# A spectral mixer and a quantised feed-forward layer on one core: the transform along h split over even and odd rows

## The chip, the core and the metric

The kernel runs on one core of a Trainium2 chip. The metric is the device time of one launch in microseconds (us). The kernel before takes 2757.5 us, the median of three runs that lie between 2753.7 and 2760.68 us. The profiled execution spans 2754.4 us, with a mean granted TensorE clock of 0.970.

The core has five instruction queues that run beside one another: TensorE (PE in the profile, with PEld for its weight loads), VectorE (DVE), ScalarE (ACT), GpSimd (POOL) and SyncE (SP), which here only issues transfers. ScalarE issues transfers too. Each queue runs in the order in which the program was written.

## The reference

The input is x with 8 images of 128 rows (h), 128 columns (w) and 96 channels. One layer is computed: a mixer in the frequency domain, then a feed-forward part in 8-bit floats, each added to its input. Cut to what matters:

```python
v = _ln_c(x)                                        # norm over the 96 channels, eps 1e-6
x_pre = soa(einsum('bhwc,mc->bhwm', v, w1))         # relu, square, scale, bias; m = 192
xf = rfft2(x_pre over h, w, norm='ortho')           # 128 x 65 frequencies
y = relu(bn(einsum('bhwc,sc->bhws', v, sp_w)))      # 48 context channels
fused = concat([v.mean(h, w), y.mean(h, w)])
r = softmax((soa(fused @ fc1.T) @ fc2.T).reshape(-1, 3, 192), axis=1)
comb = einsum('shwm,bsm->bhwm', filt, r)            # filt: three complex filters, resized from small grids
x = x + einsum('bhwm,cm->bhwc', irfft2(xf * comb), w2)

t = x as (b, 16384, 96)
h = relu(q_acc(q_acc(q_mul(ln(t)) @ q_mul(W1).T) + q_mul(b1)))   # 384 wide
y = q_acc(q_acc(q_mul(h) @ q_mul(W2).T) + q_mul(b2))
x = t + y                # q_mul: 5 exponent, 2 mantissa bits; q_acc: 5 and 10 bits
```

## The kernel before

Each image passes three streams, and the streams of neighbouring images overlap: while image b is in the last stream, b+1 is in the second and b+2 in the first.

**Stream a, `before(b)`**, goes over the columns w in 32 units of 4 columns. `load_x` brings 16 columns with h on the partitions, `measure` (L581) takes statistics per pixel, and the helper `rstd` turns them into a reciprocal root: five GpSimd steps for the variance (L591 to L595), a root on ScalarE (L600), a reciprocal on VectorE (L604), and one Newton step of four GpSimd operations (L413 to L416). `store_r` writes the factors to DRAM and `load_r` reads them back, spread over the 96 channel partitions (`rB`). `scale` (L659) multiplies the channel-major copy of x, which is stored as (c, h, w), by `rB`, and puts the product into `zT` as (c, w, h). `project` (L672) multiplies by the weights, `rectify` (L683) and `square` (L690) follow on ScalarE. `transform` (L701) is the real transform along h: for two columns at a time one product of the full 128 x 128 basis `F1` with 384 columns of `X`. `put` (L708) copies each result from PSUM with ScalarE, and `store_y` (L711) writes four columns to the DRAM tensor `Yd`, laid out as (frequency j, w, 192 channels). The order of the frequencies in `Yd` is groups of four: k, k+32 in cosine, the same in sine.

**Stream s, `spectrum(b)`**, goes over 33 groups g of four frequency rows. `load_y` reads them with w on the partitions. The 192 channels make one and a half times 128, so `pack` (L866, GpSimd) copies the last 64 channels of two rows into one tile `yb`, and `along_w` (L874) does three products for each of cosine and sine. `weigh` (L857) multiplies the resized filters by the mixing weights, `filters_of` (L887) resizes them along w in 64 x 64 tiles, and VectorE (`make` L913, `times` L916) and GpSimd (`turn_back` L923, `real_basis` L938 and L940) do the complex product. `mix_low` (L971, L984, again in 64 x 64 tiles), `mix` (L995), `mixed`, `invert` (L1011), `inverted` and `store_v` (L1021) multiply by w2, go back along w and write `Vd`.

**Stream c, `after(b)`**, goes over w again in 32 units of 4 columns, in blocks of 16. `last` (L1123) goes back along h, `residual` (L1131) adds x, `measure` and `rstd` normalise (with three more GpSimd steps for the mean, L612 to L614), `quantise` (L1151) makes 8-bit values, `turn` (L1156) and `turned` (L1166, VectorE) transpose them, `first` (L1170) makes three PSUM banks of 512, `accumulated` (L1177) copies each to 16 bits, `biased` (L1181) adds the bias and clips at zero, once for each of the three, `hidden` (L1185) rounds to 8 bits, `second` (L1192), `put8` (L1203) and `bias` (L1207) follow, and `add_up` (L1210, GpSimd) and `store` end the block. For the last image every second `quantise` runs on VectorE (L1149).

**The order.** Every piece of work is recorded by `at` with a planned time, computed from the tables `STREAMS`, `O` and `OWN` (the time of a unit plus an offset for the kind of work), and with the pieces that it needs. `in_order` sorts them by that time, moves a follower to at least a fixed `LAG` behind what it needs, and hands out six PSUM banks; a piece that needs more banks than are free is held back. The result is pinned as the order on all five engines.

Of the kernel before, what the change touches and what calls it, by code (L numbers as in the profile page):

```python
# [56 lines left out]
NG = 31  # L57
NP = 16
WB = 16
HB = WB // 2  # L60
NWB = W // WB
QW = 4
NQ = WB // QW
NU = W // QW

STREAMS = {
    "a": ((-2.3, 125.8), (125.5, 235.3), (361.7, 294.9), (654.8, 258.7), (914.4, 293.7), (1208.1, 250.0), (1549.9, 242.8), (1792.3, 246.3)),
    "s": ((145.6, 218.8), (374.7, 303.7), (677.8, 243.8), (924.7, 275.3), (1223.3, 298.2), (1520.9, 283.8), (1811.0, 258.1), (2086.7, 264.0)),
    "c": ((456.0, 260.1), (727.0, 260.5), (1018.6, 240.5), (1251.4, 323.7), (1604.0, 246.4), (1857.3, 253.2), (2101.5, 235.3), (2381.7, 138.0)),
# [4 lines left out]
        "a_load_xT": -1.97,  # L74
        "a_load_r": -5.06,
        "a_store_r": -9.58,
        "a_load_x": -10.466,
        "a_measure": -8.83,
        "a_scale": -1.29,
        "a_project_u0": 0.1,  # L80
        "a_rectify_u0": -4.22,
        "a_project_u2": 0.07,
        "a_rectify_u2": -5.38,
        "a_square": -3.56,
        "a_context": 0.88,
        "a_transform_u0": 1.37,
        "a_put_u0": 1.34,
        "a_transform_u2": 1.21,
        "a_put_u2": -5.7,
        "a_store_y": -2.773,  # L90
        "a_step": 0.26,
        "a_rstd": -4.27,
    },
    ("c", 6): {
        "c_step": 0.17,
        "c_rstd": 5.43,
        "c_quantise": 6.37,
        "c_first": 9.04,
        "c_accumulated": 8.29,
        "c_biased": 7.57,  # L100
        "c_load_v": 0.59,
        "c_last": 1.93,
        "c_residual": 1.66,
        "c_measure": -1.75,
        "c_turn": 8.21,
        "c_turned": 2.68,
        "c_hidden": 10.24,
        "c_second": 11.45,
        "c_put_blkq": 6.6,
        "c_bias": 8.21,  # L110
        "c_add_up": 7.54,
        "c_store": 8.05,
    },
    ("c", 7): {
        "c_step": 0.11,
        "c_rstd": 5.33,
        "c_quantise": 6.22,
        "c_first": 7.65,
        "c_accumulated": 2.03,
        "c_biased": 7.82,  # L120
        "c_load_v": -2.61,
        "c_last": 1.79,
        "c_residual": -0.5,
        "c_measure": -5.02,
        "c_turn": 6.63,
        "c_turned": 6.3,
        "c_hidden": 8.8,
        "c_second": 9.02,
        "c_put_blkq": 9.35,
        "c_bias": 3.04,  # L130
        "c_add_up": 9.99,
        "c_store": 3.47,
    },
    ("s", 7): {
        "s_load_y": -6.85,
        "s_load_t": -3.503,
        "s_weigh": -2.2,
        "s_pack": -2.89,
        "s_along_w_g1": -1.69,
        "s_copy_sr": -3.98,  # L140
        "s_along_w_g0": -5.22,
        "s_filters_of": -1.38,
        "s_make_dmALUsubtract": -2.12,
        "s_make_dpALUadd": -2.45,
        "s_times_t1dm00": -7.26,
        "s_times_t2dp10": -11.08,
        "s_times_t3dm01": -3.94,
        "s_times_t4dp11": -1.04,
        "s_turn_back_g0": -0.01,
        "s_turn_back_g1": -0.53,  # L150
        "s_real_basis_g0": 0.5,
        "s_real_basis_g1": -13.48,
        "s_along_w_g0_x": -1.76,
        "s_alone_z": -4.41,
        "s_filters_of_x": -1.0,
        "s_alone_t": -3.96,
        "s_alone_x": -1.27,
        "s_mix_low": 0.05,
        "s_mix": -0.12,
        "s_mixed": -3.05,  # L160
        "s_invert": 0.88,
        "s_inverted": -2.36,
        "s_store_v": -9.843,
# [3 lines left out]
T_WEIGHTS, T_CONST, T_ROWS = -112.0, -48.0, (-19.0, 94.0)  # L167

O = {
    "a_load_xT": -3.37,  # L170
    "a_load_r": -8.87,
    "a_store_r": -11.4,
    "a_load_x": -10.636,
    "a_measure": -7.71,
    "a_scale": -0.88,
    "a_project_u0": -0.28,
    "a_rectify_u0": -6.09,
    "a_project_u2": 0.13,
    "a_rectify_u2": -4.67,
    "a_square": 0.25,  # L180
    "a_context": 0.82,
    "a_transform_u0": 1.31,
    "a_put_u0": -2.63,
    "a_transform_u2": 1.05,
    "a_put_u2": -2.74,
    "a_store_y": -5.993,
    "s_load_y": -4.81,
    "s_load_t": -2.653,
    "s_weigh": -0.53,
    "s_pack": -0.19,  # L190
    "s_along_w_g1": 0.49,
    "s_copy_sr": -4.8,
    "s_along_w_g0": 0.64,
    "s_filters_of": 0.97,
    "s_make_dmALUsubtract": 0.87,
    "s_make_dpALUadd": 0.85,
    "s_times_t1dm00": -3.01,
    "s_times_t2dp10": -9.29,
    "s_times_t3dm01": -2.33,
    "s_times_t4dp11": 1.37,  # L200
    "s_turn_back_g0": 1.79,
    "s_turn_back_g1": 2.03,
    "s_real_basis_g0": 2.18,
    "s_real_basis_g1": -7.56,
    "s_along_w_g0_x": 0.15,
    "s_alone_z": -4.37,
    "s_filters_of_x": 1.5,
    "s_alone_t": -0.23,
    "s_alone_x": -3.9,
    "s_mix_low": 1.23,  # L210
    "s_mix": 1.38,
    "s_mixed": -0.75,
    "s_invert": 2.22,
    "s_inverted": 0.88,
    "s_store_v": -1.203,
    "a_step": 0.53,
    "a_rstd": -3.83,
    "c_step": 0.22,
    "c_rstd": 4.21,
    "c_quantise": 5.11,  # L220
    "c_first": 6.59,
    "c_accumulated": 5.43,
    "c_biased": 7.0,
    "c_load_v": -2.91,
    "c_last": 0.76,
    "c_residual": -1.01,
    "c_measure": 0.49,
    "c_turn": 6.04,
    "c_turned": 3.07,
    "c_hidden": 7.86,  # L230
    "c_second": 8.37,
    "c_put_blkq": 5.18,
    "c_bias": 3.81,
    "c_add_up": 8.94,
    "c_store": 3.77,
}
BANKS = 6

LAG, TRANSFER_LAG = 0.15, 2.28
# [6 lines left out]
)  # L246

# [27 lines left out]
def _constants():  # L275
# [7 lines left out]
    weight[0] = weight[L - 1] = 1.0  # L283

    rows = []
    for g in range(NG):
        k = g + 1
        rows += [k, k + 32, 64 + k, 96 + k]
    rows += [32, 96, 0, 64]

    turned = []
    for p in range(NP):
        for r in range(2):
            for g, cs in _columns(p, r):
                k = g + 1 + 32 * r if g < NG else 32 if g == NG else 64 * r
                turned.append(k + 64 * cs)
    out = {
        "F1": np.concatenate([cos, sin[1:-1]])[rows].T * norm,
# [3 lines left out]
        "CEN": np.eye(C) - 1 / C,  # L302
# [19 lines left out]

def in_order(ops):


    keys = {op.key for op in ops}
    assert len(keys) == len(ops)
    left, then, ready, held = {}, defaultdict(list), [], []
    place = {op.key: op.time for op in ops}
    for op in ops:  # L330
        needs = {k for k in op.needs if k in keys}
        left[op.key] = len(needs)
        for k in needs:
            then[k].append(op)
        if not needs:
            heappush(ready, (op.time, op.seq, op))

    free, banks, frees, order = list(range(BANKS)), {}, defaultdict(list), []
    for op in ops:
        for u in op.until:  # L340
            frees[u].append(op)
# [993 lines left out]
```

## Time and profile before

| engine | busy us | share of the span |
|---|---|---|
| PE | 2567.8 | 93% |
| PEld | 1953.0 | 71% |
| DVE | 2276.1 | 83% |
| ACT | 2233.0 | 81% |
| POOL | 2122.2 | 77% |

The transfers move 618.05 MB, 224 GB/s on the mean over the span. In the view by 40 slices PE shows 9 (90% or more busy) from the third slice to the 34th, and falls to 5 to 7 in the last three; the first slice has 4. The other engines show 6 to 9 in the middle.

A group of instructions is listed as line, engine, operation, output <- input, shapes, count | busy time in us, mean ns of one | idle time of the engine just before them, and who ended it. A product of 32-bit floats shows as two instructions. The busy time of a group is the union of its instructions, so that overlapping ones count once, while the mean counts each in full.

### The profile page before, as it was taken

How to read it: one execution, taken by the hardware profiler on the slowest of the kernel's cores; microseconds unless marked ns; L12 is line 12 of the kernel's file. 1: busy time of each engine (PE TensorE's matmuls, PEld its weight loads, DVE VectorE, ACT ScalarE, POOL GpSimd, SP SyncE). 2: the span in 40 equal slices, each digit the busy share in tenths (PEclk: the TensorE clock that was granted, in tenths of full speed). 3: DMA queues.
4: the chain of work that ended last, by engine and by line, in shares of the span. 5: the costliest groups of instructions: out<-in, count | busy, mean ns of one | idle time of the engine just before them, and what ended most of it. 6: DMA issues, size and time to landing. Idle time of an engine off the chain costs nothing.

```text
span 2754.4 us, 69406 instructions
## 1 busy us (share of the span) xinstructions
PE 2567.8 (93%) x25130; PEld 1953.0 (71%) x25130; DVE 2276.1 (83%) x5887; ACT 2233.0 (81%) x4452; POOL 2122.2 (77%) x3246
## 2 busy tenths in 40 slices
PE   4989999999999999999999999999999998999765
PEld 2668877777677777777677777777777776677433
DVE  3557667798898999889898889889889878999786
ACT  2665556699888879889998878889988997888898
POOL 1239997888788878988688969888788886889432
PEclk9899999999999999999999999999999998999896
DMA  7888777977688866878687757888777774656441
GB/s 205 263 263 253 242 224 241 287 233 251 209 255 260 252 213 196 271 242 262 220 258 245 243 171 220 273 259 257 231 239 242 230 222 147 185 178 190 149 129 62
DMA packets 480023, 618.05 MB, mean 224 GB/s; under 512 B 174542, under 2 KB 381270, under 8 KB 479658
## 3 DMA queue, kind: packets, MB, share of 16 engines
q1 hardware_dynamic: 424386, 462.60, 56.8%
q10 hardware_dynamic: 55296, 151.02, 14.7%
q8 instruction: 199, 3.26, 0.5%
q14 instruction: 142, 1.16, 0.1%
HBM read 405.36 MB, written 208.16 MB: 223 GB/s over the span
## 4 chain that ended last, share of the span: by engine, by line
PE 68%; DVE 13%; ACT 7%; POOL 4%; DMA 4%; issue 3%; SPq 1%; POOLq 0%; ACTq 0%; DVEq 0%
PE px L672 13%; PE pz L874 10%; PE py L701 10%; PE pv L995 7%; PE pf L887 6%; PE pg L1011 5%; PE ph L1170 4%; PE pk L1123 4%; PE po L1192 3%; PE pv L984 3%; DVE t L916 3%; DVE y L1181 2%; ACT h L1185 2%; ACT y L1177 2%; DVE st L581 2%
## 5 line engine op out<-in xcount | busy, mean ns | idle before, releaser
L923 POOL TENSOR_TENSOR rr<-t,t 128x390 f32<-128x390 f32 x512 | 520.4, 1017 | 60.4 <-DVE t L916 60.0
L672 PE MATMUL px<-W1S,zT 97*128 97x240 f32 x2048 | 519.4, 379 | 34.1 <-DVE zT L659 29.2
L1177 ACT CAST y<-ph 128x512 f16<-128x512 f32 x768 | 456.0, 603 | 24.2 <-PE ph L1170 22.4
L672 PEld LDWEIGHTS px<-W1S,zT 97*128 97x128 f32 x2048 | 377.2, 194 | 130.0 <-issue 33.7
L1151 ACT ACTIVATE z<-t,ln_m,ln_r 128x96 fp8e5<-128x96 f32 x960 | 461.2, 492 | 8.6 <-POOL ln_m L614 5.7
L1181 DVE TENSOR_SCALAR y<-y,b1q 128x512 f16<-128x512 f16 x768 | 427.5, 568 | 28.2 <-ACT y L1177 25.6
L683 ACT ACTIVATE rl<-px 128x480 f32<-128x480 f32 x512 | 295.7, 581 | 177.5 <-PE px L672 160.2
L701 PE MATMUL py<-X,F 128*128 128x384 f32 x1024 | 430.7, 507 | 2.1 <-ACT X L690 1.9
L1185 ACT ACTIVATE h<-y 128x1536 fp8e5<-128x1536 f16 x256 | 386.2, 1509 | 2.2 <-DVE y L1181 1.6
L659 DVE SCALAR_TENSOR_TENSOR zT<-xT,rB 96x512 f32<-96x512 f32 x256 | 339.8, 1328 | 53.1 <-DMA rB<-Rd 26.5
L874 PEld LDWEIGHTS pz<-F,yt 128*128 128x128 f32 x2080 | 301.4, 192 | 72.0 <-DVE t L1131 5.9
L1210 POOL TENSOR_TENSOR t<-t,o 128x1536 f32<-128x1536 f32 x64 | 210.1, 3282 | 167.8 <-DVE o L1207 165.8
L874 PE MATMUL pz<-F,yt 128*128 128x130 f32 x2080 | 329.0, 281 | 10.2 <-DVE t L1131 4.7
L857 POOL TENSOR_TENSOR tb<-tb,r 128x384 f32<-128x384 f32 (+1 forms) x264 | 287.0, 1087 | 59.7 <-DVE r L808 23.1
L916 DVE TENSOR_TENSOR t<-dm,pf 128x390 f32<-128x390 f32 x512 | 282.6, 552 | 43.8 <-PE pf L887 18.4
L1170 PE MATMUL ph<-zT,W1q 96*128 96x512 fp8e5 x768 | 293.5, 397 | 19.1 <-DVE zT L1166 13.9
L708 ACT COPY yst<-py 128x384 f32<-128x384 f32 x512 | 246.4, 486 | 74.3 <-PE py L701 67.8
L916 DVE TENSOR_TENSOR t<-dp,pf 128x390 f32<-128x390 f32 x512 | 280.3, 548 | 0.0
L940 POOL TENSOR_TENSOR xf<-rr 128x378 f32<-128x378 f32 x256 | 255.3, 997 | 19.7
L995 PEld LDWEIGHTS pv<-w2A,xf 128*128 128x128 f32 x2048 | 246.8, 194 | 13.6 <-issue 1.5
L995 PE MATMUL pv<-w2A,xf 128*128 128x96 f32 x2048 | 255.2, 278 | 0.0
L938 POOL TENSOR_TENSOR xf<-rr 128x390 f32<-128x390 f32 x256 | 250.1, 977 | 0.0
(126 smaller groups left out, 5210.5 us busy)
## 6 DMA issues: line engine op xcount, KB each, us to landing
Yd<-yst ACTq DMA_DIRECT2D x256, 384.0 KB
yt<-Yd SPq DMA_DIRECT2D x256, 384.0 KB
xb<-in_x SPq DMA_DIRECT2D x64, 768.0 KB
xT<-in_xT SPq DMA_DIRECT2D x128, 384.0 KB
rB<-Rd SPq DMA_DIRECT2D x128, 384.0 KB
tb<-T SPq DMA_DIRECT2D x256, 192.0 KB
Vd<-gst ACTq DMA_DIRECT2D x128, 384.0 KB
xr<-in_x SPq DMA_DIRECT2D x64, 768.0 KB
```

The costliest lines, as they stand in the source:

```text
L659: nc.vector.scalar_tensor_tensor(zTs[(b * NU + u) % NZT][:C, :, :], kept["xT", hb][:, :, w].rearrange("c h w -> c w h"), 1.0, kept["rB", h ...
L672: nc.tensor.matmul(px[:, i * (MED + SCTX) : (i + 1) * (MED + SCTX)], lhsT=zTs[(b * NU + u) % NZT][:, i0 + i, :], rhs=W1S, start=True, stop ...
L701: nc.tensor.matmul(py, lhsT=F1, rhs=kept["X", u][:, i0 : i0 + 2, :].rearrange("h w m -> h (w m)"), start=True, stop=True)
L874: nc.tensor.matmul(pz[:, u * 2 * L : (u + 1) * 2 * L], lhsT=y, rhs=F2[:, cs, :], start=True, stop=True)
L916: nc.vector.tensor_tensor(work(name, g), kept[d, g], pair(g, sign, c), ALU.mult)
L923: nc.gpsimd.tensor_tensor(kept["rr", g][:, :, 2 * i : 2 * i + 2, :], kept[ta, g], kept[tb, g][:, :, ::-1, :], op)
L995: nc.tensor.matmul(kept["pv", p, r][:, i * C : (i + 1) * C], lhsT=kept["xf", g][:, cs, r, :], rhs=w2A, start=False, stop=(i == len(_column ...
L1151: nc.scalar.activation(z, t, AF.Identity, bias=m, scale=r, saturate=False)
L1170: nc.tensor.matmul(kept["ph", u, n], lhsT=W1q[:, n * 128 : (n + 1) * 128], rhs=kept["zT", u], start=True, stop=True)
L1177: nc.scalar.copy(kept["y", u][:, n, :], kept.pop(("ph", u, n)))
L1181: nc.vector.tensor_scalar(y, y, b1q[:, n : n + 1], 0.0, ALU.add, ALU.max)
L1185: nc.scalar.activation(kept["h8", u], kept["y", u], AF.Copy, saturate=False)
```

## The change

The change has six parts; their purpose is to take work from TensorE and VectorE and to make the planned order closer to what the engines can do.

1. **The transform along h in quarter tiles.** Cosines and sines of row k and row 64-k differ over even and odd h only in sign. The columns of the input are therefore stored with the even rows on partitions 0 to 63 and the odd rows on 64 to 127 (`H_ORDER`), the basis `F1` shrinks to 64 columns, and `transform` makes four products of 64 x 64 x 384 for a unit: even and odd rows for two pairs of columns. `put` takes the even part with a sign (`SIGNS`) on ScalarE, and the new `join` on VectorE adds and subtracts the odd part.
2. **Rows paired in DRAM.** `Yd` is (pair, w, 2 x 192): k and 64-k lie side by side, so that 384 channels are contiguous and `along_w` reads three pieces of 128 straight from the tile. `pack` is gone. `store_y` becomes two transfers of 64 partitions.
3. **The norm in fewer steps.** The Newton step of four operations becomes s + v/s and a second reciprocal, with factors folded into `CEN` and into two small ScalarE scalings (`factors`) in stream c. Stream a works on 32 columns at a time, transposes the factors with TensorE (`turn_r`, `turned_r`), and writes them to DRAM in rows of 512 bytes from ScalarE's queue. `xT` and `rB` are stored as (c, w, h), so that `scale` reads contiguously.
4. **Merged biases.** One addition of 128 x 1536 in 16 bits replaces the three of 128 x 512 with a clip; `hidden` clips by using Relu instead of Copy.
5. **`turned` on ScalarE** for all images but the last. The loads of stream c come in halves with three buffers.
6. **The order.** `in_order` keeps a clock for each engine, with a table of costs, and takes the piece that can start first; the tables of planned times are new.

```diff
-                kept["xT", hb][:, :, w].rearrange("c h w -> c w h"),
+                kept["xT", hb][:, w, :],
...
-        def transform(u, i0):
-            py = kept["py", u, i0] = bank("py")[:, : 2 * MED]
-            nc.tensor.matmul(
-                py, lhsT=F1, rhs=kept["X", u][:, i0 : i0 + 2, :].rearrange("h w m -> h (w m)"), start=True, stop=True
+        def transform(u):
+            for p in range(2):
+                kept["py", u, p] = bank("py")[:, : 2 * MED]
+            for i in range(2):
+                for p in range(2):
+                    rows = slice(64 * p, 64 * p + 64)
+                    nc.tensor.matmul(
+                        kept["py", u, p][64 * i : 64 * i + 64, :],
+                        lhsT=F1[rows, :],
+                        rhs=kept["X", u][rows, 2 * i : 2 * i + 2, :].rearrange("h w m -> h (w m)"),
...
-            nc.scalar.copy(kept["yst", u][:, i0 : i0 + 2, :].rearrange("j w m -> j (w m)"), kept.pop(("py", u, i0)))
+            nc.scalar.activation(
+                kept["ev", u].rearrange("j w m -> j (w m)"), kept.pop(("py", u, 0)), AF.Identity, scale=SIGNS[:, 0:1]
+            )
+        def join(u):
+            y = kept["yst", u] = pa.tile([128, 2, 2, MED], F32, name="yst", tag="yst", bufs=3)
+            ev, od = kept.pop(("ev", u)), kept.pop(("py", u, 1)).rearrange("j (w m) -> j w m", m=MED)
+            nc.vector.scalar_tensor_tensor(y[:, :, 0, :], ev, SIGNS[:, 1:2], od, ALU.mult, ALU.add)
+            nc.vector.scalar_tensor_tensor(y[:, :, 1, :], od, SIGNS[:, 2:3], ev, ALU.mult, ALU.add)
...
         def store_y(u):
-            nc.scalar.dma_start(out=Y[b][:, u * QW : (u + 1) * QW, :], in_=kept.pop(("yst", u)))
+            for i in range(2):
+                w = slice(u * QW + 2 * i, u * QW + 2 * i + 2)
+                nc.scalar.dma_start(out=Y[b][:, w, :], in_=y[64 * i : 64 * i + 64, :, :, :].rearrange("j w p m -> j w (p m)"))
...
-        def pack(g):
-            nc.gpsimd.tensor_copy(yb, src)
...
-            newton(r, v, d, C)
+        def rest(key):
+            nc.gpsimd.tensor_tensor(v, v, kept["r", key], ALU.mult)
+            nc.gpsimd.tensor_tensor(v, v, kept.pop(("s", key)), ALU.add)
+        def again(key):
+            nc.vector.reciprocal(kept["r", key], kept.pop(("v", key)))
+        def turn_r(key):
+            nc.tensor.transpose(kept["pr", key][:SB, :128], kept["r", key], ident)
+        def store_r(key):
+            nc.scalar.dma_start(out=kept["Rd", key], in_=kept.pop(("rT", key)))
...
-            nc.vector.tensor_copy(kept["zT", u], kept.pop(("pz",) + divmod(u, NQ))[:C, :], saturate=False)
+            if b < B - 1:
+                nc.scalar.activation(kept["zT", u], pz, AF.Copy, saturate=False)
+            else:
+                nc.vector.tensor_copy(kept["zT", u], pz, saturate=False)
...
-        def biased(u, n):
-            nc.vector.tensor_scalar(y, y, b1q[:, n : n + 1], 0.0, ALU.add, ALU.max)
+        def biased(u):
+            y, b1 = kept["y", u], b1q.unsqueeze(2).to_broadcast([128, NHC, QW * 128 // BC, BC])
+            nc.vector.tensor_tensor(y, y, b1, ALU.add)
...
-            nc.scalar.activation(kept["h8", u], kept["y", u], AF.Copy, saturate=False)
+            nc.scalar.activation(kept["h8", u], kept["y", u], AF.Relu, saturate=False)
...
-            lag = TRANSFER_LAG if follower.key[1].startswith(("load", "store")) else LAG
-            place[follower.key] = max(place[follower.key], place[op.key] + lag)
+            t, k = max(start[i], free_at[e]), ops[i].banks
...
+        if e == "PE":
+            us += 0.09 * (cost.tiles != mode)
```

## The prediction

> **What bounds the kernel now.** First the busy shares, then a table of stretches, one from the middle and the last one.
>
> ```profile
> PE 2567.8 (93%) x25130; PEld 1953.0 (71%) x25130; DVE 2276.1 (83%) x5887; ACT 2233.0 (81%) x4452; POOL 2122.2 (77%) x3246
> ```
>
> ```profile
> 1300.00:1600.00 300.00, 294.09 (x2843) 224.50 (x2842) 262.19 (x677) 272.84 (x553) 248.23 (x379) 0.99 0.76 239
> 2600.00:2754.00 154.00, 94.02 (x672) 54.68 (x672) 116.10 (x349) 129.13 (x234) 48.99 (x101) 0.80 0.34 107
> ```
>
> The columns after the length are PE, PEld, DVE, ACT and POOL. In the middle PE is busy for 98% of the time. In the last 154 us ACT leads with 84% and PE drops to 61%. The chain of waits agrees: 68% of it is PE.
>
> A busy PE isn't a full PE: products overlap, and a record lasts longer than the step to the next one. So I read starts in the timeline of PE.
>
> ```profile
> 1506.72 0.38 PE L1170 MATMUL ph<-zT,W1q 96*128 96x512 fp8e5 x1
> 1507.03 0.90 PE L887 MATMUL pf<-RW,tb 52*64 52x130 f32 x24
> 1507.86 0.91 PE L701 MATMUL py<-X,F 128*128 128x384 f32 x2
> ...
> 1508.83 0.81 PE L1123 MATMUL pk<-vin,GK 128*128 128x384 f32 x2
> 1509.47 0.81 PE L1011 MATMUL pg<-V,GL 128*128 128x384 f32 x2
> 1510.12 0.38 PE L1170 MATMUL ph<-zT,W1q 96*128 96x512 fp8e5 x1
> 1510.34 0.97 PE L672 MATMUL px<-W1S,zT 97*128 97x240 f32 x4
> 1511.15 0.81 PE L1011 MATMUL pg<-V,GL 128*128 128x384 f32 x2
> ...
> 1513.41 0.81 PE L701 MATMUL py<-X,F 128*128 128x384 f32 x2
> 1514.06 0.97 PE L672 MATMUL px<-W1S,zT 97*128 97x240 f32 x4
> ```
>
> A product of 384 columns in 32 bits takes 0.65 us to the next start (1509.47 to 1510.12), L672 0.81 for two products, L1170 0.22. The group L887 in 64 x 64 tiles takes 0.83. Before it, L1170 needs 0.31 instead of 0.22: entering the tiles costs 0.09. Three full-size products of 130 columns (L874) take 0.67 in the same timeline, so twelve one after another would need 2.7; L887's twelve take 0.83. Four tiles run at once, with about 0.09 for each entry and exit.
>
> With these steps an image costs PE, per unit of columns: 1.62 (L672) + 1.30 (L701) + 0.65 (L1123) + 0.66 (L1170) + 0.22 (L1156) + 0.51 (L1192) = 4.96, times 32 = 159. Per group: 1.34 + 0.83, times 33 = 72 with the entries ahead of them. Per pair of groups: 0.18 + 0.76 (L984) + 1.77 (L995) + 1.30 (L1011), times 16 = 64. With entries and the small products it comes to about 297 us, 2378 for eight images and the setup. In the listing of the tile Vd the last store starts at 2573.3; the first L672 is at 42.9 in the chain. In these 2530 us PE had some 2300 us of work (2378 less 73 for the rest of stream c and some setup): **91% of its real capacity**. Hence PE is the bound, but not tight: 9% goes to small waits between five nearly full engines.
>
> **What the Trainium skill says.** "TensorEngine Tiling (Array Packing)", section Tiling Modes: tiles run independently, and changing the tiling mode drains TensorE. The trace agrees: four at once, 0.09 us at a change. The same page, Performance Considerations, warns that tiling doesn't speed up the evacuation of PSUM and can make it the bound; here that is `put` and `join`, and nothing before the change shows it. "VectorE: DVE Perf Modes", the section with the perf-mode tier table: 16-bit `tensor_tensor` reaches 2x at best, `tensor_scalar` 4x. L1207 below, 1536 elements in 1054 ns, fits 2x.
>
> **The change part by part.**
>
> ```profile
> L1181 DVE TENSOR_SCALAR y<-y,b1q 128x512 f16<-128x512 f16 x768 | 427.5, 568 | 28.2 <-ACT y L1177 25.6
> L659 DVE SCALAR_TENSOR_TENSOR zT<-xT,rB 96x512 f32<-96x512 f32 x256 | 339.8, 1328 | 53.1 <-DMA rB<-Rd 26.5
> L708 ACT COPY yst<-py 128x384 f32<-128x384 f32 x512 | 246.4, 486 | 74.3 <-PE py L701 67.8
> L1166 DVE CAST zT<-pz 96x512 fp8e5<-96x512 f32 x256 | 173.5, 678 | 32.7 <-PE pz L1156 32.5
> L866 POOL COPY yb<-yt 128x256 f32<-128x256 f32 x264 | 138.5, 525 | 9.8 <-DMA yt<-Yd 9.8
> L1207 DVE TENSOR_TENSOR o<-o,b2q 128x1536 f16<-128x1536 f16 x64 | 67.4, 1054 | 16.1 <-ACT o L1203 15.3
> L805 DVE SCALAR_TENSOR_TENSOR lg<-lg,SEL 128x192 f32<-128x192 f32 x16 | 8.0, 501 | 0.6
> ```
>
> *PE.* A unit's transform goes from two full products (1.30) to four tiles side by side (0.65): 256 x 0.65 = 166 us off. In PE's instruction order the changes between full and tile products rise from 786 to 1058; 272 x 0.09 = 24 us back. 32 transposes of the norm's factors, unseen before: between 0.06 (a quarter of L1156's 0.22) and 0.22 (a product of L874); I take 0.13, 4 us. Net **-136 us**, 2378 to 2242. This lies on the path. If the tiles didn't overlap in full, the saving would vanish; L887 and L984 speak against it.
>
> *ACT.* Steps between starts in the timeline are shorter than the durations: 0.37 for L708, 0.48 for L1177. Half of L708's copies go (256 x 0.37 = 95 us). The other half gets a scale for each partition: the skill's page "ScalarE: Activation LUTs", section What ACT_TABLE_LOAD costs, prices such a pointer at 93 ns, so 256 x 0.1 = 25 us more; L1151, with two pointers, takes 492 ns for 96 elements, which fits. `turned` comes over: 224 x 0.48 = 108 us. The small norm steps add about 20. Net **+58 to +66**: by steps 2113 to about 2179, 272 us an image against PE's 280. ACT also issues 672 transfers instead of 384, and these bring a wait: formerly `store_y` followed ACT's own copy, now it needs `join` on VectorE. Queued behind it are L1177, L683 and `hidden`, and PE's banks wait for those. The order puts a median of 5.2 us of ACT's own work between `put` and its store (formerly 1.1), so I cost it at nothing, and keep 1 us for each unit as the upper end.
>
> *DVE.* `biased`: 768 x 568 becomes 256 of L1207's kind, 427 to 270, -158. `scale` reads contiguously: L1166 handles 512 elements in 678, so 256 x 0.68 = 174, -166. `turned` leaves, -152. `join` is new: 512 of 384 elements, between 550 (L1131, the same size) and 700 (L805 plus 192 more elements at 1.0 ns, the slope from L1131 to L1166); I take 600, +307. 64 more reciprocals (L604, 243): +16. Net **-150**, 2276 to about 2125. Off the path unless a wait for `join` shows.
>
> *POOL.* `pack` -138. The norm, by the groups of 128 x 16, falls from about 363 to 220, -140. 2122 to about 1845; hidden beside PE in the middle.
>
> *Transfers.* The bytes stay. `load_y` moves pieces of 1536 bytes instead of 768, `store_r` rows of 512 bytes instead of pieces of 32. The DMA share of 0.76 isn't the bound; cost and gain nothing.
>
> *The end.* After 2573.3 the trace has 181 us. The last blocks follow each other every 17.5 us (starts of L1210), with ACT full; 8 x 17.5 = 140. None of ACT's large steps there changes. In the new order two units fewer are left after the last `inverted` (-8), with the new small scalings +3: 176.
>
> *The sum.* PE's work from 43 us to the last store falls from 2300 to about 2165. At the same 91%: 2165 / 0.91 = 2380, ending at 2423; with 176 about **2600 us**.
>
> **The rivals.**
> 1. *The new order packs better.* Its planner knows costs and banks, where the old one knew a fixed lag, and DVE and POOL have more slack. At 95% of PE: 2165 / 0.95 = 2279, plus 43 and 176 = 2500. For it: the 9% in small waits. Against it: ACT has 3% more work, and each transform holds two of six PSUM banks until `put` and `join` are done.
> 2. *ACT takes over as the bound.* 2179 less 140 of the end is 2039, plus 288 more transfer issues at 0.1 (29); a queue that waits for PE, DVE and POOL in turn may be only 84% full: 2068 / 0.84 = 2462, plus 219 = 2680. For it: ACT was at 81% and grows while PE shrinks.
> 3. *ACT is held by `join`.* With 1 us lost at each of 256 stores: 2324 / 0.90 = 2582, plus 219 = **2801**, slower. For it: ACT's queue is strictly in order, and 196 stores carry a VectorE wait. Against it: the 5.2 us of distance.
>
> **How the numbers follow.** The forecast 0.53, rival 1 0.24, rival 2 0.14, rival 3 0.09. The range reaches from rival 1 to just above rival 2: 2505 to 2700; about 0.1 lies below and 0.12 above. The unknown costs (`join` at 550 to 700, the pointer) move DVE and ACT by some 40 us each off the path, and the range covers that. Faster 0.88 (the first three with a little taken off), same 0.03, slower 0.09.
>
> **What would show it.** The transform's eight records should take about 0.65 us from start to start between tile groups, 0.83 between full products. `scale` near 680 ns, the merged addition near 1050, `join` near 600, `put` near 580. PE's work over the stretch should stay near 91%. ACT's idle time ahead of `rectify` and `accumulated` should still be ended by PE; if it is ended by VectorE, rival 3 holds. The last blocks should still come every 17.5 us. A transform of 1.3 us, or a PE share below 85% with a full ACT, would make the prediction wrong.

## The result and the profile after

| kernel | median us | runs | ratio to before, with its 95% interval |
|---|---|---|---|
| before | 2755.6 | 2753.28 to 2760.68 | |
| after | 2784.4 | 2780.62 to 2789.84 | 1.0104 (1.0078 to 1.0129) |

The change makes the kernel 1% slower. The prediction said 2600 us. The profiled execution of the changed kernel spans 2785.4 us.

First, the busy shares of the changed kernel. Below them is its table of stretches, with the same columns as before: length, PE, PEld, DVE, ACT, POOL, then the granted clock of PE, the share of the transfers and GB/s.

```profile
PE 2532.9 (91%) x26202; PEld 1856.8 (67%) x26202; DVE 2256.3 (81%) x5727; ACT 2266.5 (81%) x4548; POOL 1925.3 (69%) x2438
```

```profile
0.00:200.00 200.00, 137.46 (x581) 76.96 (x581) 115.21 (x441) 81.18 (x144) 35.73 (x95) 0.84 0.80 234
1300.00:1600.00 300.00, 283.89 (x3030) 211.73 (x3029) 259.14 (x634) 271.30 (x555) 225.15 (x279) 0.98 0.77 232
2600.00:2785.00 185.00, 122.42 (x773) 71.57 (x772) 124.48 (x318) 152.33 (x282) 55.36 (x82) 0.69 0.36 113
```

In the middle, records of PE cover 283.89 us of 300, where they covered 294.09 before. DVE, ACT and POOL are no fuller than they were either (259.14, 271.30 and 225.15 us against 262.19, 272.84 and 248.23). A lighter PE was the aim, but nothing else took up the time.

Next the groups of instructions that the change touches, in the page and in the listings for ACT and DVE (busy us, mean ns of one, then the idle time ahead of them and who ended it).

```profile
L864 PE MATMUL py<-X,F 64*64 64x384 f32 x2048 | 237.4, 522 | 12.1 <-ACT X L848 5.2
L874 ACT ACTIVATE ev<-py,SIGNS 128x384 f32<-128x384 f32 x256 | 148.1, 580 | 55.8 <-PE py L864 34.3 <-DMA Rd<-rT 5.1 <-DVE st L735 2.3
L841 ACT ACTIVATE rl<-px 128x480 f32<-128x480 f32 x512 | 290.4, 573 | 152.8 <-PE px L830 116.4 <-DMA yt<-Yd 4.6 <-DVE t L1102 4.0
L1413 DVE TENSOR_TENSOR y<-y,b1q 128x1536 f16<-128x1536 f16 x256 | 304.0, 1189 | 87.3 <-ACT y L1408 86.6
L817 DVE SCALAR_TENSOR_TENSOR zT<-xT,rB 96x512 f32<-96x512 f32 x256 | 245.6, 966 | 23.1 <-PE px L830 13.6 <-DMA rB<-Rd 8.2 <-DMA xT<-in_xT 0.7
L882 DVE SCALAR_TENSOR_TENSOR yst<-py,SIGNS,ev 128x384 f32<-128x384 f32 x256 | 156.0, 609 | 0.0
L881 DVE SCALAR_TENSOR_TENSOR yst<-ev,SIGNS,py 128x384 f32<-128x384 f32 x256 | 154.3, 603 | 68.0 <-ACT ev L874 64.4 <-PE pk L1309 1.9 <-ACT rl L841 1.0
```

The transform is L864: its busy time falls from 430.7 us (the same tile at L701 before) to 237.4. `put` (L874) takes 580 ns and the two halves of `join` 603 and 609. Two operations on VectorE are much longer than predicted: the merged addition (L1413) with 1189 ns and `scale` (L817) with 966.

**Work and lost time.** A busy share can't tell where the 2785 us went, so I added up PE's work by stage: each record at its step from start to start (0.65 us for a transform in tiles, 0.81 for two products of `project`, and so on as in the prediction), and 0.09 for each entry into or exit from the tiles. The lost time is the stretch less that work. The steps are estimates, so a single figure is good to some 20 us and a difference between two kernels to some 10. For the kernel before this gives 2411 us of work, where the prediction's sum had 2378.

| kernel | span | PE's work | lost in 0 to 500 | 500 to 2200 | from 2200 |
|---|---|---|---|---|---|
| before | 2754.4 | 2411 | 79 | 100 | 164 |
| after | 2785.4 | 2280 | 138 | 191 | 176 |

PE has 131 us less to do, against 136 predicted. But it loses 162 us more: 59 at the start, 91 in the middle, 12 at the end. The experiments look for these 162 us. A first hint: from 500 to 2200 us PE has 71 us of idle stretches over 0.15 us after the change, and 64.5 of them are ended by ScalarE; before, they were 35 us, 19.5 ended by VectorE and 13.1 by ScalarE.

### The profile page after: what moved, and what is told of

Same layout as the page of the kernel before. It is cut to its first block, busy times and chain, and to the rows that moved or that the text cites. A ratio compares the mean times of both kernels' runs of the same rounds, so it can differ in the third digit from the quotient of the medians.

```text
span 2785.4 us, 71364 instructions
## 1 busy us (share of the span) xinstructions
PE 2532.9 (91%) x26202; PEld 1856.8 (67%) x26202; DVE 2256.3 (81%) x5727; ACT 2266.5 (81%) x4548; POOL 1925.3 (69%) x2438
## 5 line engine op out<-in xcount | busy, mean ns | idle before, releaser
L1059 PE MATMUL pz<-F,yt 128*128 128x130 f32 (+1 forms) x3136 | 447.3, 284 | 4.6 <-ACT y L1408 2.4
L1376 ACT ACTIVATE z<-t,ln_m,ln_r 128x96 fp8e5<-128x96 f32 x960 | 411.6, 471 | 48.4 <-issue 23.0
L1059 PEld LDWEIGHTS pz<-F,yt 128*128 128x128 f32 (+1 forms) x3136 | 408.1, 193 | 64.2 <-ACT y L1408 11.9
L1408 ACT CAST y<-ph 128x512 f16<-128x512 f32 x768 | 416.3, 596 | 32.4 <-PE ph L1401 23.0
L841 ACT ACTIVATE rl<-px 128x480 f32<-128x480 f32 x512 | 290.4, 573 | 152.8 <-PE px L830 116.4
L1413 DVE TENSOR_TENSOR y<-y,b1q 128x1536 f16<-128x1536 f16 x256 | 304.0, 1189 | 87.3 <-ACT y L1408 86.6
L1401 PE MATMUL ph<-zT,W1q 96*128 96x512 fp8e5 x768 | 263.3, 406 | 44.1 <-ACT y L1408 14.0
L855 POOL TENSOR_TENSOR sacc<-sacc,rl 128x192 f32<-128x192 f32 x248 | 163.0, 657 | 199.5 <-ACT rl L841 193.2
L1102 DVE TENSOR_TENSOR t<-dm,pf 128x390 f32<-128x390 f32 x512 | 263.6, 553 | 3.9 <-PE pf L1073 1.2
L817 DVE SCALAR_TENSOR_TENSOR zT<-xT,rB 96x512 f32<-96x512 f32 x256 | 245.6, 966 | 23.1 <-PE px L830 13.6
L864 PE MATMUL py<-X,F 64*64 64x384 f32 x2048 | 237.4, 522 | 12.1 <-ACT X L848 5.2
```

What stands on the lines that cost most here:

```text
L841: nc.scalar.activation(kept["rl", u][:, i0 : i0 + 2, :].rearrange("h w m -> h (w m)"), kept.pop(("px", u, i0)), AF.Relu)
L1059: nc.tensor.matmul(pz[lo : lo + n, u * 2 * L : (u + 1) * 2 * L], lhsT=y[:, m0 : m0 + n], rhs=F2[:, cs, :], start=True, stop=True)
L1102: nc.vector.tensor_tensor(work(name, g), kept[d, g], pair(g, sign, c), ALU.mult)
L1376: nc.scalar.activation(z, t, AF.Identity, bias=m, scale=r, saturate=False)
L1401: nc.tensor.matmul(kept["ph", u, n], lhsT=W1q[:, n * 128 : (n + 1) * 128], rhs=kept["zT", u], start=True, stop=True)
L1408: nc.scalar.copy(kept["y", u][:, n, :], kept.pop(("ph", u, n)))
```

## Experiments: issuing the stores

A line of ACTq is ScalarE's queue issuing a transfer; I call this a trigger. These lines are from the timeline of ACT in the changed kernel.

```profile
1409.40 1.05 ACT L1408 CAST y<-ph 128x512 f16<-128x512 f32 x2
1410.11 0.45 ACTq L888 DMA_DIRECT2D Yd<-yst  x1
1410.34 0.60 ACT L1395 ACTIVATE zT<-pz 96x512 fp8e5<-96x512 f32 x1
1410.60 0.61 ACTq L888 DMA_DIRECT2D Yd<-yst  x1
1411.25 0.26 ACT L799 COPY rT<-pt 32x128 f32<-32x128 f32 x1 [0.31 <-issue]
1411.54 0.32 ACTq L803 DMA_DIRECT2D Rd<-rT  x1
1411.91 0.35 ACT L778 ACTIVATE ln_s<-ln_v 128x32 f32<-128x32 f32 x2 [0.40 <-ACT rT L799]
```

The two triggers of one `store_y` take 0.45 and 0.61 us of the queue. L1395, with its step of 0.48, runs beside them. The next instruction, L799, starts only when the second trigger has ended, at 1410.60 + 0.61. The reason given for L799's idle time is "issue": it waits for nothing that the profile shows. The kernel before, in the same view:

```profile
1408.08 1.50 ACT L1185 ACTIVATE h<-y 128x1536 fp8e5<-128x1536 f16 x1
1408.22 0.33 ACTq L711 DMA_DIRECT2D Yd<-yst  x1
1409.46 0.59 ACT L1177 CAST y<-ph 128x512 f16<-128x512 f32 x1
```

One trigger of 0.33 us lies inside `hidden`'s 1.50 us, and L1177 follows at once. The listings of the tile Yd give the sizes (minimum, median and maximum in ns); first before, then after.

```profile
L711 ACTq DMA_DIRECT2D Yd<-yst x256: 326/326/1084, 51.1 to 2276.4; - x128
```

```profile
L888 ACTq DMA_DIRECT2D Yd<-yst x512: 452/490/2220, 63.3 to 2329.7; - x171
```

The median of after mixes two kinds: the first trigger of a `store_y` has a median of 453 ns and the second, right behind it, 609. A pair takes 1.06 us. From 700 to 2200 us I summed the time between two ACT instructions beyond the step of the first, wherever a trigger lies between them: 15 us before, 121 after. Gaps without a trigger make 248 us before and 90 after.

**sp_store: the triggers leave ScalarE.**

```diff
-                nc.scalar.dma_start(out=Y[b][:, w, :], in_=y[64 * i : 64 * i + 64, :, :, :].rearrange("j w p m -> j w (p m)"))
+                nc.sync.dma_start(out=Y[b][:, w, :], in_=y[64 * i : 64 * i + 64, :, :, :].rearrange("j w p m -> j w (p m)"))
```

> The changed kernel with the two store transfers of each unit (Yd) issued from SyncE's queue instead of ScalarE's; planner, tables and the order of all computing work are the same. Theory T (triggers): in the changed kernel a unit's two store transfers hold ScalarE's queue for 0.45 + 0.61 us, where the one transfer of before took 0.33, and the ScalarE instruction behind them starts late; over the middle 1500 us these gaps sum to 121 us against 15. T expects the gaps to go and the time to fall by 80 to 160 us, to 2620 to 2700. Rival O (the new order itself packs badly, whatever the queue of the stores): 2784 within 15. Rival P (TensorE is still the bound): 2784 within 15.

2709.8 us (0.984, 0.9815 to 0.9864), 75 us less than after. The time lost behind triggers falls from 121 to 29 us, and PE's lost time in the middle from 191 to 129. It is the same compute in the same order, so having the triggers on ScalarE costs 75 us.

**one_store: one trigger of 128 partitions on ScalarE.** `Yd` is laid out so that the store is one transfer; `load_y` becomes two of 64 partitions on SyncE.

```diff
-        Y[b] = dram.tile([64, 128, 2 * MED], F32, name="Yd", tag="Yd")
+        Y[b] = dram.tile([128, 64, 2 * MED], F32, name="Yd", tag="Yd")
...
+            nc.scalar.dma_start(out=Y[b][:, 2 * u : 2 * u + 2, :], in_=y.rearrange("j w p m -> j w (p m)"))
...
+                nc.sync.dma_start(out=yt[64 * i : 64 * i + 64, :, :], in_=halves[i, :, 2 * g : 2 * g + 2, :])
```

> The changed kernel with Yd laid out so that a unit is stored in one transfer of 128 partitions from ScalarE, as before the change; the load of a group becomes two transfers of 64 partitions on SyncE and the rows of the basis along w are reordered on the host. Order of the computing work the same. T expects one trigger of about 0.33 us in place of 1.06, the gaps behind triggers down to some 15 to 30 us in the middle 1500, and 2640 to 2710. O and P: 2784 within 15.

2720.86 us (0.9887, 0.986 to 0.9914). The trigger is back at a median of 327 ns. So it is the pair of transfers of 64 partitions on ScalarE, not `store_y` on ScalarE as such, that makes most of the cost. With the store still on ScalarE, 64 of the 75 us come back, so the gain of sp_store isn't due to SyncE's queue.

**before_two: the reverse, in the kernel before.**

```diff
-            nc.scalar.dma_start(out=Y[b][:, u * QW : (u + 1) * QW, :], in_=kept.pop(("yst", u)))
+            y = kept.pop(("yst", u))
+            for i in range(2):
+                nc.scalar.dma_start(out=Y[b][64 * i : 64 * i + 64, u * QW : (u + 1) * QW, :], in_=y[64 * i : 64 * i + 64, :, :])
```

> The kernel before with the store of each unit split into two transfers of 64 partitions, issued by ScalarE; nothing else. T expects about 0.7 us more of ScalarE's queue for each of 256 units; ScalarE had slack there and TensorE was the bound, so a part is hidden: 2755 plus 15 to 90. O and P: 2755 within 10.

2781.23 us (1.0101, 1.0078 to 1.0124), some 27 us more than before. The split alone makes the kernel before as slow as the changed one. It costs less there, which fits the 248 us of other gaps that ScalarE had to hide it in, against 90 after the change.

**sp_planned: sp_store, and the planner knows it.**

```diff
-    "store_y": Cost("ACT", 0.18, 2, 1.11),
+    "store_y": Cost("SP", 1.0, 2, 1.11),
```

> The changed kernel with the stores of Yd issued from SyncE and the planner told so (1.0 us of SyncE for a unit's two triggers). In the run with the stores moved behind the planner's back 2710 was measured. T expects a little more: 2680 to 2705, since SyncE's order is planned now. O expects 2600 to 2670.

2691.94 us (0.9767, 0.9749 to 0.9785): the fastest version, 2.3% under the kernel before and 92 us under the changed one. The page of sp_planned, and its middle:

```profile
PE 2482.9 (92%) x26202; PEld 1835.3 (68%) x26202; DVE 2247.7 (84%) x5727; ACT 2265.8 (84%) x4548; POOL 1944.4 (72%) x2438
```

```profile
1300.00:1600.00 300.00, 293.38 (x3179) 220.17 (x3178) 268.54 (x648) 283.15 (x581) 237.11 (x290) 1.00 0.82 246
```

ACT's busy time is that of after within 1 us. The same operations now fit in less time: 283.15 us of 300 instead of 271.30.

**costed: after, with truer prices in the planner.** `store_y` at the measured 1.06 us of ScalarE, the merged addition at 1.04.

```diff
-    "store_y": Cost("ACT", 0.18, 2, 1.11),
+    "store_y": Cost("ACT", 1.06, 2, 1.11),
-    "biased": Cost("DVE", 0.86, shared=True),
+    "biased": Cost("DVE", 1.04, shared=True),
```

> The changed kernel with two costs in the planner's table set to what its trace shows: 1.06 us of ScalarE for a unit's two store triggers instead of 0.18, and 1.04 us for the merged addition instead of 0.86. Nothing else. T expects little, since the triggers still take ScalarE's time: 2750 to 2785. O (the order was wrong because its costs were wrong) expects most of the loss back: 2650 to 2720.

2841.14 us (1.031, 1.0294 to 1.0325), against both expectations: 57 us slower than after. PE's lost time in the middle grows from 191 to 227 us. The time behind triggers does fall, by the same kind of sum from 121 to about 80 us, but ScalarE's other gaps grow by some 80. Here a planner that knows the price found no better order; taking the work off the queue did.

## Experiments: what TensorE's work is worth

With the triggers off ScalarE the kernel is at 2710 or 2692 us, still some 100 us over the forecast. So I doubled, halved and moved single loads.

**twice: the changed kernel with every tile product of `transform` issued twice**, 256 x 0.65 = 166 us more for PE.

```diff
-            for i in range(2):
+            for i in (0, 1, 0, 1):
```

> The changed kernel with each of the four tile products of a unit's transform issued twice into the same place: 166 us more work on TensorE (256 x 0.65), nothing else. P (TensorE is the bound) expects at least 140 of these in the time, 2925 or more. T (ScalarE with its triggers is the bound, TensorE has 12% of its time free in the middle) expects less than half: 2800 to 2865. O likewise, with the same range.

2885.93 us (1.0484, 1.0458 to 1.051): 101 us for 166, a slope of 0.61. This lies between the two expectations. TensorE is neither off the path nor the only thing on it.

**twice_head: the same for the first two images only**, 42 us.

```diff
-            for i in range(2):
+            for i in [i for i in range(2) for _ in range(2 if b < 2 else 1)]:
```

> The changed kernel with the tile products of transform issued twice for the first two images only, which nearly all lie in the first 500 us: 64 x 0.65 = 42 us more work for TensorE there. If TensorE isn't what sets the pace of the start, so that a saving of transform cannot show there either, the time rises by 5 to 20 us: 2789 to 2804 us. If it sets the pace there as much as elsewhere (twice: 101 us for 166, so 0.61 of the work), it rises by some 25 us or more: 2810 to 2830 us.

2809.31 us (1.021, 1.0192 to 1.0227), 25 us for 42 by the medians (29 by the ratios): a slope of 0.6 or a little more again. My idea that the start hides the transform's work altogether fell.

**before_half: half of the transform's products left out of the kernel before.** Its order is unchanged on all engines, and only PE's work shrinks, by the same 166 us that the quarter tiles save.

```diff
-                py, lhsT=F1, rhs=kept["X", u][:, i0 : i0 + 2, :].rearrange("h w m -> h (w m)"), start=True, stop=True
+                py[:, :MED], lhsT=F1, rhs=kept["X", u][:, i0, :], start=True, stop=True
...
-            nc.scalar.copy(kept["yst", u][:, i0 : i0 + 2, :].rearrange("j w m -> j (w m)"), kept.pop(("py", u, i0)))
+            nc.scalar.copy(kept["yst", u][:, i0 : i0 + 2, :], kept.pop(("py", u, i0))[:, :MED].unsqueeze(1).to_broadcast([128, 2, MED]))
```

> The kernel before, in the same order, with one column instead of two in each product of transform; put copies the one result to both places, as long as before. It leaves out half of the transform, so its output is another one. It takes 512 x 0.325 = 166 us off TensorE, as the quarter tiles do, and touches nothing else. By the prediction's step (the same 91% of a smaller work) this is worth 166 / 0.91 = 182 us: 2575 us, say 2560 to 2600. By the slope of twice and twice_head (0.6 of the work shows): 100 us, 2640 to 2675 us. If other engines or the fixed order hold the kernel, still less: above 2690 us.

2687.78 us (0.9769, 0.9738 to 0.98): 67 us for 166, a slope of 0.40 (55 to 72 us by the interval). In its timeline a transform of one column takes 0.33 us to the next start, so the saving itself is whole. The middle of before_half:

```profile
1300.00:1600.00 300.00, 282.66 (x2891) 228.39 (x2891) 268.71 (x687) 270.37 (x554) 248.74 (x373) 0.98 0.79 243
```

PE's records cover 94%, DVE 90%, ACT 90%, POOL 83%. Nothing took over as the one bound. PE's idle stretches over 0.15 us from 500 to 2200 us grow from 35 to 67 us, and two engines end them about equally: VectorE 34.9 us, ScalarE 29.1. The same sum of work and lost time as above (here it makes the work left out 175 us, within its error):

| kernel | span | PE's work | lost in 0 to 500 | 500 to 2200 | from 2200 |
|---|---|---|---|---|---|
| before | 2754.4 | 2411 | 79 | 100 | 164 |
| before_half | 2685.5 | 2236 | 121 | 164 | 164 |
| sp_planned | 2685.1 | 2275 | 124 | 116 | 170 |
| after | 2785.4 | 2280 | 138 | 191 | 176 |
| twice | 2881.3 | 2446 | 106 | 147 | 183 |

Taking work off PE, and doing nothing else, raises the lost time by 42 us at the start and 64 in the middle. So a lighter PE alone can account for most of the 59 us that the change loses at the start; twice, in the new order, takes 32 of them back. What before_half can't tell is what an order planned anew for the lighter PE would have gained.

**sp_twice: twice, on sp_planned.**

```diff
-            for i in range(2):
+            for i in (0, 1, 0, 1):
```

> sp_planned with every tile product of transform issued twice, as in twice, 166 us more work for TensorE, in the same order otherwise. With ScalarE's queue free of the store's triggers, TensorE should be more of a bound than in the changed kernel: if its slope rises to 0.8 or more, 2825 to 2860 us. If the slope is 0.6 here too, 2780 to 2805 us, and the slope doesn't depend on the triggers.

2798.02 us (1.0161, 1.014 to 1.0181): 106 us for 166, a slope of 0.64. The slope hardly depends on the triggers.

**head_light: fewer bytes at the start.** In the first 500 us of the changed kernel the transfers' share is 0.78 to 0.91 in stretches of 100 us, so I suspected them. For the first two images only half of `xT` is loaded, and `scale` uses that half twice; the factors `rB` are shortened in the same way.

```diff
-            nc.sync.dma_start(out=t, in_=xT[b, hb, :, :, :])
+            n = HB // 2 if b < 2 else HB
+            nc.sync.dma_start(out=t[:, :n, :], in_=xT[b, hb, :, :n, :])
```

> The changed kernel, in which scale of the first two images reads only the first four of every eight columns of xT and of the norm's factors, and uses them twice; the other halves are not loaded. That leaves out 32 transfers' worth of bytes for each of the two tensors, 2 x 2 x 3.1 = 12.6 MB, and no work of any compute engine. Theory H (the first 500 us are bound by transfers, so a third of the transform's saving cannot show there): at the 270 to 290 GB/s of that stretch 12.6 MB are 43 to 47 us, so 2735 to 2762 us. Rival (the start is held by latencies, by VectorE or by the order): within 10 us of the changed kernel, 2774 to 2794 us.

2775.76 us (1.0075, 1.0051 to 1.01): 9 us for 12.6 MB, where 43 to 47 were expected. The bytes aren't what sets the pace there.

**sb16: the norm over 16 columns again, on sp_planned.**

```diff
-SB = 32
+SB = 16
```

> sp_planned with the norm of stream a over 16 columns at a time again instead of 32 (SB = 16), planned anew. The first product of stream a waits for the norm's factors; in the changed kernel it starts 9.5 us later than in the kernel before (52.4 against 42.9). If the late start is carried through the start of the kernel, this gains 5 to 12 us, less the extra small steps of the norm (32 more of each, about 0.16 us each on ScalarE and VectorE and 2 us on GpSimd): 2675 to 2690 us. If the start is absorbed by the wait for all of the first image, as the order has it: 2688 to 2705 us.

2745.83 us (0.9969, 0.9957 to 0.9981), 54 us slower than sp_planned, outside both expectations. At the start it loses 8 us less, in the middle 45 more, so what it shows is mostly another order, and the norm's part stays undecided.

## Experiments: the other engines and the order

**sp_dve and dve_kept: `turned` on VectorE for every image.** Both have the stores on SyncE, as in sp_store. The first is planned anew; the second keeps the order of sp_store.

```diff
-            if b < B - 1:
-                nc.scalar.activation(kept["zT", u], pz, AF.Copy, saturate=False)
-            else:
-                nc.vector.tensor_copy(kept["zT", u], pz, saturate=False)
+            nc.vector.tensor_copy(kept["zT", u], pz, saturate=False)
```

> The changed kernel with the stores of Yd issued from SyncE, and in addition turned back on VectorE for all images as before the change; the planner is told so and plans anew. Theory A (with the triggers gone ScalarE, at 0.92 to 0.95 of the middle, is still the bound, since turned gave it 108 us): 2650 to 2690. Rival D (VectorE would be next, it gets 0.6 us for 224 units, 134 us): 2700 to 2760.

> sp_store with turned on VectorE for every image, like sp_dve, but the order of all work stays the one of sp_store (the planner still counts turned on ScalarE). It takes 224 x 0.48 = 108 us off ScalarE and puts 152 us on VectorE. If sp_dve lost 67 us because VectorE is the next limit, this loses much the same: 2740 to 2790 us. If sp_dve lost them because its order was planned anew, this stays close to sp_store's 2709.8 or below it: 2650 to 2715 us.

sp_dve takes 2776.62 us (1.0078, 1.0061 to 1.0096) and dve_kept 2713.66 (0.9851, 0.9827 to 0.9876). The same operations on the same engines differ by 63 us: the order planned anew costs it, not VectorE. Against sp_store's 2709.8, dve_kept shows nothing, although 108 us of steps left ScalarE. The middle of dve_kept:

```profile
1300.00:1600.00 300.00, 293.26 (x3179) 220.09 (x3173) 284.61 (x697) 274.01 (x550) 244.49 (x296) 0.99 0.83 253
```

VectorE is at 95% here and ScalarE at 91%; in sp_store it is 89% and 94%. Either way the time is the same. As the work only changes sides, a gain on ScalarE and a loss on VectorE could cancel; this pair doesn't separate them.

**vec_kept: one `quantise` in eight on VectorE, in the order of sp_planned.**

```diff
-            return b == B - 1 and i % 4 in (1, 3, )
+            return i % 4 in (1, 3) if b == B - 1 else i % 8 == 0
```

> sp_planned with one quantise in eight on VectorE for the first seven images, in the same order: ScalarE gets 112 x 0.36 = 40 us less, VectorE 27 us more. In sp_planned ScalarE is busy for about 95% of the middle and TensorE for 98%. If ScalarE is still one of the limits: 2650 to 2682 us. If TensorE alone is the limit: 2685 to 2700 us. If VectorE (91% busy) is the next limit, it is slower: above 2700 us.

2695.13 us (0.9776, 0.9748 to 0.9803), no difference from sp_planned. It takes 40 us off ScalarE and puts 27 on VectorE. So ScalarE's remaining work, as opposed to the triggers, doesn't seem to bound the kernel by itself.

**nudge: sp_store with a cost of `join` that is 4% higher in the planner.**

```diff
-    "join": Cost("DVE", 1.06),
+    "join": Cost("DVE", 1.1),
```

> sp_store in which only the planner's cost of join is 1.10 us instead of 1.06; the instructions are the same, in another order. Theory N (the plan is sensitive to any nudge, whatever it says of the engines, since the tables of planned times were fitted to one set of costs): more than 15 us from sp_store's 2709.8, likely slower, 2725 to 2790 us. Rival (the plan changes smoothly with its costs): 2700 to 2720 us.

2705.05 us (0.9816, 0.9785 to 0.9847). Of the neighbouring pairs of ScalarE instructions 2111 of 4547 stay neighbours, so the order does change, and it costs nothing. But costed reorders more (1116 pairs stay), and one nudge doesn't say how far larger new orders scatter. The 57, 54 and 63 us of costed, sb16 and sp_dve may or may not be such scatter.

**old_planner: the changed kernel, with the new tables of times under the old `in_order`.** The function and its two constants `LAG` and `TRANSFER_LAG` come from the kernel before.

```diff
-            t, k = max(start[i], free_at[e]), ops[i].banks
+            lag = TRANSFER_LAG if follower.key[1].startswith(("load", "store")) else LAG
+            place[follower.key] = max(place[follower.key], place[op.key] + lag)
```

> The changed kernel with its tables of planned times, but ordered by the function of before (sorted by planned time, a fixed lag, no engine clocks). Stores on ScalarE as in the changed kernel. Rival O (the new order packs worse than the old) expects less than 2784, about 2720 to 2760. T (the triggers, not the order) expects no gain: 2784 to 2950, since the planned times were made for the other function.

4131.84 us (1.4985, 1.496 to 1.501). The new tables mean nothing to the old planner, so this run doesn't tell what the new order is worth.

## Why the prediction was wrong

**The sizes held.** PE's work fell by 131 us, not 136. `put` took 580 ns as said, 94 more than L708's 486 before, where the pointer was priced at 93; `join` took 603 and 609 for 600. ACT's busy time rose by 34 us, POOL's fell by 197. The idle time ahead of `rectify` (L841) is still ended by PE in the main, 116.4 us of 152.8. The end is right too: the last store of Vd starts at 2606.2 us, so 179 us follow it, where I said 176. On VectorE two terms were mis-sized: the merged addition at 1189 ns for 1054, and `scale` at 966 for 680. Together that is some 108 us, most of the way from the predicted 2125 us to VectorE's 2256. dve_kept puts 152 us more on VectorE, for 108 less on ScalarE, without a loss, so this is hardly the cause.

**First failed step: "At the same 91%".** The prediction divided the smaller work by the old share, which turned 135 us of saved work into 150 us of time (2530 to 2380). before_half measures that step alone: 67 us for 166, a slope of 0.40 where the step assumed 1.1. For 135 us this makes 54, so the step was 96 us too generous. By the slope that added work shows in the new order (0.61 and 0.64) it would be 82 to 86 us, and the step still 64 too generous. The share is not a property of the kernel that stays; when PE gets lighter, it waits more for others that are 83 to 90% busy. By the sum of steps, PE did 86% of its capacity between its first product of stream a and the last store of Vd after the change (2198 us of work in 2554), 89% in sp_planned and 92% before. Rival 2, ScalarE as the new bound, is nearer to the changed kernel than its 2680 us suggest: with the triggers, ScalarE's queue is taken for all but 90 of the 1500 us from 700 to 2200, 94%, and it ends 64.5 of the 71 us of PE's idle stretches. But twice adds 101 us, so it isn't the only bound, and once the triggers are gone dve_kept and vec_kept show no single engine in PE's place.

**Second failed step: "ACT also issues 672 transfers instead of 384".** The forecast counted these issues and gave them no price. What it cost at nothing was the wait for `join`, and that held; the triggers themselves stand in no term of the forecast, and rival 2 put them at 0.1 us. A price was in the trace: 326 ns each in the listing of Yd before, which makes 94 us for 288 more. The measured one is higher still, as a pair takes 1.06 us where one trigger took 0.33, some 190 us more of the queue over 256 units. sp_store measures what of this shows in the time, 75 us; sp_planned, with an order planned for it, gains 92. before_two shows the same cost in the kernel before, at some 27 us.

**The sum.** 2757.5 - 54 + 75 gives 2779 us; 2784.4 was measured. And 2757.5 - 54 = 2704 lies beside the versions without the triggers (2692 and 2710). That it comes out so closely is in part luck: the slope of 0.40 was measured in the order of the kernel before and the triggers in the order after, and with the slope of 0.61 the same sum gives 2750, 34 us short. The new norm, the merged additions and the halved loads were not taken out one by one, so what they gain or lose is not known.

**Rival 3** named 2801 us, the nearest of the four times, but by another mechanism: ACT held by `join`. In the waits of ACT after the change, the waits for the tile yst of `join` are these:

```profile
ACT sr L1095 <- DVE yst L882: 2.6, 1, 2.6
ACT rl L841 <- DVE yst L882: 2.5, 1, 2.5
ACT V L1192 <- DVE yst L882: 1.7, 1, 1.7
```

Some 7 us in all. The distance in the order did what the prediction said; the queue was held by its own issuing. That its number came so near is luck.

**Rival 1**, the better packing, is not borne out: sp_store and sp_planned, without the triggers, lose 129 and 116 us in the middle, more than the 100 before. The new order isn't shown to be worse either, since before_half loses 164 there.

**What stays open:** why orders planned anew with larger changes in the costs (costed, sb16, sp_dve) came out 54 to 63 us slower. That the tables of planned times were fitted to one set of costs would explain it, but no run shows it.

## What to carry to other kernels

When several engines are all over 80% busy, don't divide the saved work by the old share of the leading one: measure the slope first, by halving or doubling that work in the unchanged order. Price every transfer that an engine issues by its own line in the trace, multiply by the count, and look at what is queued behind it; a change that splits a transfer on a busy compute queue should move it to an idle queue in the same step. And when an order is planned from a table of costs, time each new plan on its own: in costed a truer cost gave a slower order.

## What the runs showed of the hardware

- **Cutting a store in two by partitions made each trigger dearer.** One trigger for the 128 partitions of `Yd` takes a median of 326 ns on ScalarE. In before_two, with half of the bytes in rows of the same length, the first of two takes 453 and the second, right behind it, 609. SyncE shows it in the loads: 360 ns for 128 partitions in after, 593 for 64 in one_store. Few partitions alone aren't the reason, as the trigger of `Rd`, 32 partitions and 16 KB, takes 324 ns (L803 in after); what sets the price was not separated. The Trainium skill, "DMA: Bandwidth & Descriptors", section Issuing engines are not separate DMA queues, says that initiating transfers on several engines saves only the sequencer's time, usually small beside the transfer. Here that time, on a queue with no room, is what sp_store wins its 75 us from.
- **GpSimd slows VectorE, but not in every operation.** In the trace of after, `scale` takes 0.67 us on the mean when no GpSimd record overlaps it (40 times) and 1.02 when one does (216 times); the merged addition 0.95 and 1.25. The two halves of `join`, with one of their inputs in PSUM, take 0.60 to 0.61 either way. The Trainium skill, "GPSIMD Engine Reference", section Specifications, says that GpSimd shares its memory interfaces (to SBUF) with VectorE and contends when an instruction there has two inputs in SBUF; the trace agrees in all four. The predicted 680 ns were those of an undisturbed `scale`. How much GpSimd loses was not measured.
- **A lighter TensorE gets a lower clock at the start.** In the first 200 us the granted clock is 0.92 before, 0.85 in before_half, 0.84 after, and 0.97 in twice. Two products of `project` (four records) show it in the changed kernel, first after an idle stretch of 7.87 us and then with none right before them:

```profile
170.03 1.94 PE L830 MATMUL px<-W1S,zT 97*128 97x240 f32 x4 [7.87 <-DVE yst L882]
193.78 1.08 PE L830 MATMUL px<-W1S,zT 97*128 97x240 f32 x4
```

The Trainium skill, "TensorE: Matmul & The Clock Gate", section Part 1: The HAM clock gate, describes a gate that halves the clock after idle stretches; the trace agrees with 1.94 us against 1.08. A part of the saved work at the start may be lost in this way; how much was not separated.
